# Layer 0 of a four-layer transformer stack: where the first norm runs, where the context's products stand, and what the last maxima are read from

## The chip, the cores and the metric

The kernel runs on one core of one Trainium2 chip. The metric is the device time of one execution in microseconds, the median of several runs. A core has a matrix engine (TensorE, PE in the profile; PEld is its weight load), VectorE (DVE), ScalarE (ACT), GpSimd (POOL) and SyncE (SP), whose queue issues most DMAs. Each takes its own instructions in order, and they wait for each other through semaphores.

## The reference

Eight samples of 256 tokens with 320 channels pass through four layers. The change is in layer 0 alone:

```python
h = attention(layer_norm(x, ln1_g, ln1_b), layer_norm(x, ln1_g, ln1_b), Wq1, Wk1, Wv1, Wo1, bo1, heads)
x = x + h
h = attention(layer_norm(x, ln2_g, ln2_b), ctx, Wq2, Wk2, Wv2, Wo2, bo2, heads)
x = x + h
x = x + geglu_ff(layer_norm(x, ln3_g, ln3_b), Wff1, bff1, Wff2, bff2)

def attention(x, ctx, Wq, Wk, Wv, Wo, bo, heads):
    q, k, v = fq_sym(x @ Wq), fq_sym(ctx @ Wk), fq_sym(ctx @ Wv)   # then 20 heads of 16
    w = fq_zero(softmax(q k^T * dh ** -0.5))
    return (w v, heads merged) @ Wo + bo
```

`fq_sym(x)` divides by `max(abs(x)) / 127`, rounds, and multiplies again; the maximum is over the whole tensor, all eight samples. `fq_zero` does the same with `max(w) / 255`. So within each attention nothing can be rounded before the last sample's queries and keys are projected, and no weight can be rounded before the last sample's softmax is known.

## The kernel before

Everything is held on the core. A sample is 2 tiles of 128 tokens. Each attention of layer 0 is a `Quant` object (`s` for self, `c` for cross) and goes through these passes:

- Projections. `project_all` (L1207) for `s`; `keys_all`, `values_all` (L1273) and `queries_all` (L1284) for `c`. After each product, ACT copies it from PSUM to SBUF, and `top` (L1201) has DVE reduce the largest absolute value into a column of `am`. For the last sample, `before` reads these maxima from PSUM in pieces; `am` has two more columns for them.
- `steps` (L1319), the first barrier of an attention. DVE reduces `am`; `all_max` (L485) goes over the partitions by two small transposes on PE (L489, L495) with DVE in between; then the step sizes follow.
- `whole` (L1339) rounds a sample's queries and keys: tk (L1347) and tq (L1350) scale and add 1.5*2^23, then L1353 and L1357 subtract it again and write two masked copies of the keys, and L1363 or L1365 the queries. With `fast` (sample 0, and sample 1 of `c`), DVE does the keys, GpSimd tq, and ACT the queries' last step; otherwise GpSimd does all.
- `tops_all` (L1407): scores on PE (L1422), their row maxima on DVE (L1425). `sums_all` (L1477): scores again, exponentials on ACT (L1473), sums on PE (L1488).
- `weight_steps` (L1514), the second barrier: the smallest sum over everything, by `all_max`, and a logarithm of all sums on ACT (L1518).
- `out_all` (L1547): `shift` (L1536) folds the sums into the row maxima; then, per group of heads, scores (L1466), exponentials, rounding on DVE (L1581), products with the values (L1563), and per sample the output projection and the addition to x (L483).

`weave` (L649) interleaves generators: each part has the round in which it begins, and every round takes one step of each living part. The order of an engine's instructions follows from this order of the program and from the framework, which takes work that is ready by its own model, the earliest in the program first. While `s.out_all()` runs, `c.queries_all()` normalises, turns and projects sample by sample (`norm`, `turn`, `project`), with the rounds of each sample in a table, `at`. The norm, `normed` (L296), takes statistics on DVE, a power on GpSimd (L310), and then L313, x minus mean times rstd, on DVE or on the engine given by `on`.

`context_steps` (L700) computes keys and values of the context for later layers and writes them to memory: a generator named `ahead`, each step a product with the context (L728), ACT copies into a staging tile, and DMAs on SP. The keys' staging tile, `kst`, has one buffer. One step is taken before `c.steps()`, 21 during `c`'s maxima and sums, at every second round (`paced`), and the rest during `c.out_all()`. PSUM offers three pairs of banks (`pair`) for all these products.

## Time and profile before

| | |
|---|---|
| median of 3 runs | 2235.7 us (2229.62 to 2238.51) |
| the profiled execution | 2235.43 us, its span 2233.4 us, mean granted clock 0.965 |
| self-attention: projections, then barrier | to 106, 106 to 110 us |
| its maxima and sums, barrier, output | 110 to 257, to 263, to 396 us |
| cross-attention: barrier, maxima and sums | 409 to 414, to 546 us |
| its barrier and output | to 553, to 675 us |
| all that follows (feed-forward, three layers) | 675 to 2233 us |

In the timeline a row has the start and the length in us, the engine, the line, the operation, what it writes and reads, how many instructions are merged, and in brackets the idle time of the engine before it and what ended it. In the windows a row has a stretch, the busy time of each engine in it with the number of instructions, the granted TensorE clock (1.00 is full speed), the DMA engines' share and GB/s.

### The profile page before, as it was taken

To read this page: it belongs to the slowest core of one execution; us is meant where nothing else is said; L and a number is where in the kernel's file an instruction comes from. 1 tells how busy PE (TensorE), PEld (TensorE's weight loads), DVE (VectorE), ACT (ScalarE), POOL (GpSimd) and SP (SyncE) were. 2 spreads that over 40 slices of the span, in tenths; PEclk is the share of its full clock that TensorE was granted. 3 is DMA by queue.
4 is the path that set the end of the run, shared out by engine and by line. 5 is a ranking of instruction groups with operands and counts; after the bars stand their busy time and mean duration, and the time that the engine had idled before them with its cause. 6 is when DMAs were issued, how large, how long until landed. Compare 5 with 4: busy or idle time off the path is not lost.

```text
span 2233.4 us, 38265 instructions
## 1 busy us (share of the span) xinstructions
PE 2044.5 (92%) x16413; PEld 1201.3 (54%) x16413; DVE 1117.4 (50%) x1698; ACT 825.7 (37%) x1252; POOL 357.9 (16%) x365
## 2 busy tenths in 40 slices
PE   6889878898899999999999999899999799999997
PEld 5643345554444555465555555554555455666664
DVE  4388677555752221335655667611121466556465
ACT  2347878467532121124444443411201233222221
POOL 1092066601411000000000001100000100000100
PEclk9989889898889999999999999999999899999999
DMA  4000000642110000020000001100000201000000
GB/s 117 17 12 2 1 1 4 167 111 57 55 53 28 1 0 1 1 92 2 2 2 22 27 25 35 47 1 0 1 1 2 68 25 32 12 24 26 23 19 16
DMA packets 79303, 63.21 MB, mean 28 GB/s; under 512 B 48410, under 2 KB 68318, under 8 KB 78622
## 3 DMA queue, kind: packets, MB, share of 16 engines
q1 hardware_dynamic: 75070, 57.06, 9.3%
q10 hardware_dynamic: 4064, 3.71, 0.6%
q8 instruction: 129, 2.11, 0.4%
q14 instruction: 40, 0.33, 0.1%
HBM read 42.61 MB, written 17.37 MB: 27 GB/s over the span
## 4 chain that ended last, share of the span: by engine, by line
PE 75%; DVE 16%; ACT 5%; issue 3%; DMA 1%; POOL 1%; SPq 0%; ACTq 0%; DVEq 0%; POOLq 0%
PE pf L120 13%; PE pf L584 13%; PE pf L132 9%; PE pa L120 7%; PE pa L447 6%; PE pf L430 4%; PE pa L584 3%; PE pf L139 3%; PE pf L385 3%; DVE negm L1425 3%; PE pf L1466 3%; PE pf L728 3%; DVE rs L455 2%; PE pa L1488 2%; DVE negm L392 2%
## 5 line engine op out<-in xcount | busy, mean ns | idle before, releaser
L436 ACT ACTIVATE e<-pf 128x1024 f32<-128x1024 f32 (+2 forms) x176 | 158.3, 944 | 234.9 <-PE pf L430 227.8
L392 DVE TENSOR_REDUCE negm<-pf 128x4 f32<-128x1024 f32 (+4 forms) x224 | 188.1, 886 | 108.8 <-PE pf L385 108.8
L584 PE MATMUL pf<-xTf,ff 128*128 128x512 f32 x512 | 232.4, 601 | 5.2 <-DVE negm L392 5.2
L455 DVE RECIPROCAL rs<-pa 128x256 f32<-128x256 f32 x88 | 152.2, 1745 | 144.0 <-PE pa L447 144.0
L477 POOL TENSOR_TENSOR xb<-x_sb,brow 128x640 f32<-128x640 f32 x40 | 62.2, 1555 | 792.2 <-DVE x_sb L483 748.2
L1473 ACT ACTIVATE e<-pf,sc_s 128x1024 f32<-128x1024 f32 x160 | 169.6, 1116 | 49.4 <-PE pf L1466 42.6
L1425 DVE TENSOR_REDUCE negm<-pf 128x4 f32<-128x1024 f32 (+2 forms) x128 | 143.3, 1134 | 68.1 <-PE pf L1422 61.4
L611 DVE SCALAR_TENSOR_TENSOR hT<-pf,cols_sb,gl 128x512 f32<-128x512 f32 x64 | 48.0, 751 | 256.8 <-ACT gl L610 254.5
L120 PE MATMUL pf<-ff,hT 128*128 128x320 f32 x640 | 174.4, 434 | 0.0
L584 PEld LDWEIGHTS pf<-xTf,ff 128*128 128x128 f32 x512 | 94.9, 191 | 125.2 <-issue 119.8
L120 PEld LDWEIGHTS pf<-ff,hT 128*128 128x128 f32 x640 | 120.9, 190 | 55.5 <-issue 6.1
L430 PE MATMUL pf<-qT,kT 32*128 32x256 f32 (+1 forms) x1280 | 122.3, 411 | 21.9 <-DMA qT<-nT 12.8
L610 ACT ACTIVATE gl<-pf,cols_sb 128x512 f32<-128x512 f32 x64 | 43.9, 687 | 248.0 <-PE pf L584 248.0
L385 PE MATMUL pf<-kT,qT 32*128 32x120 f32 (+1 forms) x1920 | 114.8, 329 | 18.3 <-ACT e L436 18.1
L120 PE MATMUL pa<-o,oT 128*128 128x320 f32 x352 | 105.4, 441 | 15.2 <-DVE oT L456 14.1
L385 PEld LDWEIGHTS pf<-kT,qT 32*128 32x128 f32 x1920 | 84.9, 189 | 58.4 <-ACT e L436 27.7
L1466 PE MATMUL pf<-Q,K 32*128 32x256 bf16 (+1 forms) x960 | 90.5, 294 | 25.3 <-DVE negm L1425 13.2
L639 POOL TENSOR_TENSOR xb<-x_sb,brow 128x640 f32<-128x640 f32 x16 | 25.1, 1566 | 543.1 <-DVE x_sb L644 528.7
L447 PE MATMUL pa<-e,v 128*32 128x256 f32 (+1 forms) x1280 | 105.2, 388 | 2.3 <-ACT e L436 1.7
L1581 DVE TENSOR_SCALAR w<-e 128x1024 bf16<-128x1024 f32 (+2 forms) x128 | 87.4, 691 | 37.5 <-ACT e L1473 36.3
L430 PEld LDWEIGHTS pf<-qT,kT 32*128 32x128 f32 (+1 forms) x1280 | 68.7, 183 | 68.3 <-issue 37.3
L132 PE MATMUL pf<-xT,q 128*128 128x256 f32 x384 | 101.0, 392 | 0.4 <-ACT e L436 0.2
(287 smaller groups left out, 3448.1 us busy)
## 6 DMA issues: line engine op xcount, KB each, us to landing
ff<-in_L_xattn_Wff_dram SPq DMA_DIRECT2D x1, 2560.0 KB
qT<-nT SPq DMA_DIRECT2D x160, 4.0 KB
ff<-in_L_xattn_ff_w_dram SPq DMA_DIRECT2D x1, 2560.0 KB
out_dram<-x_sb SPq DMA_DIRECT2D x16, 160.0 KB
kd_cross<-kst SPq DMA_DIRECT2D x8, 300.0 KB
vd_cross<-vst SPq DMA_DIRECT2D x8, 300.0 KB
vd_both<-vst SPq DMA_DIRECT2D x8, 300.0 KB
kT<-kd_cross SPq DMA_DIRECT2D x8, 300.0 KB
```

What stands on the lines that cost most here:

```text
L120: self.nc.tensor.matmul(out, l, r, start=i == 0, stop=i == len(pairs) - 1)
L132: self.nc.tensor.matmul(o, *t[c], start=start and c == 0, stop=stop and c == n - 1, skip_group_check=True)
L385: nc.tensor.matmul(s[j // 2][:, j % 2, o : o + nk], qT[r : r + PAD, g, t * P : (t + 1) * P], kT[r : r + PAD, g, :nk], start=True, stop=True,)
L392: nc.vector.tensor_reduce(negm[:, n, 2 * i : 2 * i + 2, g0 : g0 + len(gs), :].rearrange("p j g t -> p j (g t)"), sv[:, :, :, k0:k1], AX.X, ...
L430: nc.tensor.matmul(s[j // 2][:ks, j % 2, o : o + N], kT[r : r + PAD, g, c * ks : (c + 1) * ks], qT[r : r + PAD, g, :], start=True, stop=True,)
L436: nc.scalar.activation(e[:ks, 2 * i : 2 * i + 2, :n], s[i][:ks, :, :n], AF.Exp, scale=scale)
L447: nc.tensor.matmul(o[j * PAD : (j + 1) * PAD, what * N : (what + 1) * N], w, es[g][:ks, j, c * N : (c + 1) * N], start=first and c == 0 an ...
L455: nc.vector.reciprocal(rs, o[:, N:])
L584: ins = nc.tensor.matmul(*args, **kw)
L1425: nc.vector.tensor_reduce(negm[:, 2 * h : 2 * h + 2, gs[0] : gs[-1] + 1, :].rearrange("p j g t -> p j (g t)"), s[:, :, : len(gs) * TPB * n ...
L1466: nc.tensor.matmul(s[at // 2][:ks, at % 2, o : o + N], l, m, start=not shift and o == 0, stop=shift and o + N == n, skip_group_check=True,)
L1473: nc.scalar.activation(e[:ks, :, :n], ps[:ks, :, :n], AF.Exp, scale=self.sc[:ks, 9:10])
```

## The change

- In `queries_all`, the norm of sample 0 goes to DVE (before, only the last sample's did). All samples have the same rounds, five apart, so the last two no longer overlap, and the pass has 44 rounds instead of 40.
- The maxima of the last sample are taken from the SBUF copies, like the others'; `am` has 8 columns instead of 10.
- In `whole`, tk is always GpSimd's; with `fast`, DVE does tq and the queries' last step, and ACT and the constant `magic` are no longer used. Only sample 0 is fast.
- In `out_all`, the last values are taken one group per round, and the last sample's output in two rounds instead of one.
- Two steps of `c.values_all()` are taken after `s.weight_steps()`, ahead of the output pass; three follow from round 44 (before: from round 41), and three, not five, in `c`'s maxima.
- A second step of `ahead` is taken between `c.steps()` and `c.whole(0)`, and 20 instead of 21 in the weave that follows.

```diff
         def norm(b):
-            x[b] = k.normed(b, self.ln, on=nc.gpsimd if b + 1 < B else None)
+            x[b] = k.normed(b, self.ln, on=nc.gpsimd if 0 < b < B - 1 else None)
...
-            if b + 1 == B:
-                self.top(0, b + m, ps[:, 0, :N])
-            elif m == 2:
+            if m == 2:
                 self.top(0, b, self.q[b])
...
-        at = {b: [5 * b + i for i in (0, 3, 6, 7, 8)] for b in range(B - 2)}
-        at[B - 2] = [5 * B - 10 + i for i in (0, 3, 4, 5, 7)]
-        at[B - 1] = [5 * B - 10 + i for i in (3, 6, 7, 8, 9)]
-        for r in range(5 * B):
+        todo = {0: norm, 3: turn, 6: lambda b: project(b, 0), 7: lambda b: project(b, 1), 8: lambda b: project(b, 2)}
+        for r in range(5 * B + 4):
...
-            if b + 1 < B:
-                self.top(0, b, q)
-                self.top(1, b, kt)
-                continue
-
-            for i, ps in enumerate((pq, pk)):
-                self.top(i, b, ps[:, :, :N])
-            for i, ps in enumerate((pq, pk)):
-                self.top(i, B, ps[:, i, N:])
+            self.top(0, b, q)
+            self.top(1, b, kt)
...
-        to.tensor_scalar(tk[:, : 3 * nk], kt, sc[:, 7:8], MAGIC, ALU.mult, ALU.add)
+        nc.gpsimd.tensor_scalar(tk[:, : 3 * nk], kt, sc[:, 7:8], MAGIC, ALU.mult, ALU.add)
...
-        nc.gpsimd.tensor_scalar(tq, q, sc[:, 6:7], MAGIC, ALU.mult, ALU.add)
+        to.tensor_scalar(tq, q, sc[:, 6:7], MAGIC, ALU.mult, ALU.add)
...
-        if fast:
-            nc.scalar.activation(qh.rearrange("p c n -> p (c n)"), tq, AF.Identity, bias=k.magic)
-        else:
-            to.tensor_scalar(qh.rearrange("p c n -> p (c n)"), tq, MAGIC, None, ALU.subtract)
+        to.tensor_scalar(qh.rearrange("p c n -> p (c n)"), tq, MAGIC, None, ALU.subtract)
...
-            for _ in self.whole(b, self.cross and b == 1):
+            for _ in self.whole(b):
...
-        for r in range(rounds * B + 2):
+        for r in range(rounds * B + 4):
...
-            while len(todo) > (2 if b < B else 0):
+            if len(todo) > (2 if b < B else 0):
                 values(*todo.pop(0))
...
-                if r == rounds * B + 1:
-                    d, left = B, 0
...
-                k.weave((0, s.out_all()), (8, c.queries_all()), (5 * B + 1, islice(v, 3)))
+                for _ in range(2):
+                    next(v)
+                k.weave((0, s.out_all()), (8, c.queries_all()), (5 * B + 4, islice(v, 3)))
...
             c.steps()
+            next(ahead)
             for _ in c.whole(0, True):
                 pass
...
-                (1, k.paced(islice(ahead, 21), 1)),
+                (1, k.paced(islice(ahead, 20), 1)),
```

More of the change, by code (lines that the diff above doesn't have):

```diff
@@ L181, in open_quant @@
             nc.gpsimd.memset(self.place[:, g, 15 + g : 30 : G], 1.0)
-        self.magic = pool.tile([P, 1], F32, name="magic")
-        nc.gpsimd.memset(self.magic, -MAGIC)
         self.fill = pool.tile([P, 1], F32, name="fill")
@@ L1194, in __init__ @@
         n = "c" if cross else "s"
-        self.am = pool.tile([P, 3, B + 2], F32, name=f"am_{n}")
+        self.am = pool.tile([P, 3, B], F32, name=f"am_{n}")
         nc.gpsimd.memset(self.am, 0.0)
@@ L1202, in top @@
         self.k.nc.vector.tensor_reduce(
-            self.am[: src.shape[0], i, b : b + 1], src, AX.XY if len(src.shape) > 2 else AX.X, ALU.max,
-            apply_absolute_value=True,
+            self.am[: src.shape[0], i, b : b + 1], src, AX.XY if i == 2 else AX.X, ALU.max, apply_absolute_value=True
         )
@@ L1300, in project @@
             nc.scalar.copy(self.q[b][:, m * N : (m + 1) * N], ps[:, 0, :N])
-            if b + 1 == B:
-                self.top(0, b + m, ps[:, 0, :N])
-            elif m == 2:
+            if m == 2:
                 self.top(0, b, self.q[b])
-        at = {b: [5 * b + i for i in (0, 3, 6, 7, 8)] for b in range(B - 2)}
-        at[B - 2] = [5 * B - 10 + i for i in (0, 3, 4, 5, 7)]
-        at[B - 1] = [5 * B - 10 + i for i in (3, 6, 7, 8, 9)]
-        for r in range(5 * B):
+        todo = {0: norm, 3: turn, 6: lambda b: project(b, 0), 7: lambda b: project(b, 1), 8: lambda b: project(b, 2)}
+        for r in range(5 * B + 4):
             for b in range(B):
-                for i, n in enumerate(at[b]):
-                    if n == r:
-                        norm(b) if i == 0 else turn(b) if i == 1 else project(b, i - 2)
+                if r - 5 * b in todo:
+                    todo[r - 5 * b](b)
             yield
@@ L1520, in weight_steps @@
         least = k.small.tile([P, 1], F32, tag="least", name="least")
-        nc.vector.tensor_reduce(least, self.am[:, 0, :B], AX.X, ALU.min)
+        nc.vector.tensor_reduce(least, self.am[:, 0, :], AX.X, ALU.min)
         nc.vector.reciprocal(part[:, 0:1], least)
@@ L1524, in weight_steps @@
         if self.cross:
-            nc.vector.tensor_reduce(part[:, 1:2], self.am[:, 2, :B], AX.X, ALU.max)
+            nc.vector.tensor_reduce(part[:, 1:2], self.am[:, 2, :], AX.X, ALU.max)
             k.all_max(most, part)
```

## The prediction

> **What bounds the kernel now.** I read the page, then the chain of waits, then the timeline around the three barriers of layer 0, where a maximum over all partitions must be known before the next pass can start. The page first: what is the bound, and where does the granted clock fall?

> ```profile
> span 2233.4 us, 38265 instructions
> ...
> PE 2044.5 (92%) x16413; PEld 1201.3 (54%) x16413; DVE 1117.4 (50%) x1698; ACT 825.7 (37%) x1252; POOL 357.9 (16%) x365
> ...
> PEclk9989889898889999999999999999999899999999
> ```

> PE is busy 92% of the span and 75% of the chain. Everything the diff touches ends by 675 us, so the other 1558 us stay. Two stretches before that hold PE back. The first is in the timeline of the first attention's output pass:

> ```profile
> 290.59 6.66 POOL L313 TENSOR_SCALAR xh<-x_sb,mv,rstd 128x320 f32<-128x320 f32 x2
> ...
> 297.31 1.33 PE L330 MATMUL pf<-ident,xh 128*128 128x128 f32 x5 [2.77 <-POOL xh L313]
> ...
> 300.79 2.12 ACT L1473 ACTIVATE e<-pf,sc_s 128x1024 f32<-128x1024 f32 x2
> ...
> 301.93 0.69 DVE L1581 TENSOR_SCALAR w<-e 128x1024 bf16<-128x1024 f32 x1 [5.91 <-ACT e L1473]
> ...
> 396.88 0.45 DVE L313 TENSOR_SCALAR xh<-x_sb,mv,rstd 128x320 f32<-128x320 f32 x1 [0.82 <-POOL rstd L310]
> ```

> The norm of sample 0 takes 6.66 us on GpSimd; PE stands before its transposes and everything queued behind them, and ACT and DVE run dry. The same instruction on DVE takes 0.45 us (last row). The chain has these 6.67 us. The second stretch is the start of the cross-attention's maxima (two views: windows, columns after the length are PE, PEld, DVE, ACT, POOL busy, granted clock, DMA share, GB/s; then the timeline):

> ```profile
> 412.00:414.00 2.00, 0.00 (x0) 0.00 (x0) 2.00 (x7) 1.61 (x4) 1.78 (x2) 0.95 0.54 134
> ...
> 414.30:428.00 13.70, 11.59 (x65) 6.81 (x65) 6.00 (x10) 4.24 (x10) 13.19 (x12) 0.50 0.39 126
> ...
> 430.00:432.00 2.00, 2.00 (x10) 1.40 (x10) 0.66 (x2) 0.42 (x1) 2.00 (x3) 0.78 0.39 154
> ```

> ```profile
> 407.88 2.58 PE L728 MATMUL pf<-ctxT,ck 128*128 128x240 f32 x12
> ...
> 414.45 0.84 PE L1422 MATMUL pf<-K,Q 32*128 32x120 bf16 x16 [3.03 <-DVE K L1353]
> ...
> 415.22 4.96 PE L728 MATMUL pf<-ctxT,ck 128*128 128x240 f32 x12
> ...
> 421.95 4.96 PE L728 MATMUL pf<-ctxT,ck 128*128 128x240 f32 x12 [1.23 <-DVE negm L1425]
> ...
> 427.98 2.49 PE L120 MATMUL pf<-v,ctxT 128*120 128x320 f32 x4 [0.74 <-DVE negm L1425]
> ...
> 436.42 1.34 PE L120 MATMUL pf<-v,ctxT 128*120 128x320 f32 x4 [1.25 <-DVE negm L1425]
> ```

> After 3 us without work, PE runs at half clock from 414 to about 431: the 12 products of a key step take 4.96 us where they took 2.58 before. DVE and ACT wait for PE there, so this is PE's stretch.

> **Part 1, the first norm on DVE.** rstd is there at 290.48. Two L313 rows on DVE are 0.9 us, so the transposes can start near 292 instead of 294.1 and 297.3. Behind them ACT finishes its exponential at 294.4 and makes xT (2.03 us), so the next round's exponentials start at about 296.4, not 300.79: **-4.4**. [...] The rows say 3.3 us against 0.45, and I go by them. DVE is busy without a gap from 263 to 296, so its 0.9 us may come off the gain: -3.5 to -4.9.

> **Part 2, whole() for sample 0 (both passes).** The key's rounding moves to GpSimd; the query's two steps come to DVE from GpSimd and ACT. First attention: before, DVE did 0.62 + 1.15 + 1.00 (L1347, L1353, L1357) from 107.94 to 110.78, and the first score reduction started at 111.00. Now it does tq (0.62, by L1347), qh (1.15, by L1353 of the same size), kh 1.15 and 1.00: one operation more in the same queue, ahead of the reductions. **+1.1** (0.6 if qh fits into the 1.2 us in which GpSimd makes tk, 1.6 if all are slowed). The reductions follow each other every 1.13 us there and set the pace, so it passes on. Cross: 0.62 to 0.98 for tq, then 0.93 to 1.15 for qh, 0.92, 0.33 from 412.05: about 415.3 instead of 414.45, +0.85 (0.2 to 1.6), counted in part 4. Sample 1 of the cross pass goes wholly to GpSimd: 0.56 + 0.90 + 1.49 + 1.08 + 2.13 = 6.2 us behind sample 0's tk, done by 419.5; its scores are due at 428 at the earliest. GpSimd's queue then ends near 456 instead of 451.7, with each later sample needed well after it is made. Hidden; if the cover were gone it would be up to 5 us.

> **Part 3, two value products ahead of the output pass.** They fill PE's gap at 257 to 263 (1.27 us each), ahead of or between the two transposes of the maximum. That route has 0.7 us of slack, since ACT's logarithm ends at 260.4. Their copies (0.42) follow the logarithm and cost nothing; their maxima, 2 x 0.49 on DVE, are placed ahead of shift(0), the chain 260.53 to 263.29: **+0.8** (0 to 1.5). DMAs: none.

> **Part 4, a key step in the gap of c.steps.** It issues 12 matmuls, ACT's puts (2.7 us) and two kd_cross writes on SP. The matmuls fill 410.6 to 414; with a part before the second transpose, as where the same line lay around it at 547 (0.6 us later): **+0.5**. Behind SP's writes stand only loads for later layers. The kst tile has one buffer: bytes of the first step move until 415.0, so ACT's second puts run 415.2 to 417.9, and a step takes 2.7 + 2.1 = 4.85 us, the fourth done at 427.5 (in before, 435.6). Out of the stretch go one step at 4.96, two value products at 1.27 (2.5), and the half clock on what remains: the next step 4.96 to 2.58, scores 1.85 to 1.03, a value product 2.49 to 1.27, 0.3 of the fourth step, together 4.7. That is 12.2 of PE's time. Walked through with three PSUM pairs (a pair is free when ACT or DVE has read it), the score unit of 444.47 comes at 436.6, with a 2.0 us step more behind it: 7.9 + 2.0 = **-9.9**, the later start of 0.85 included (bounds -4 and -11.4). [...] The rows show half clock for 16 us at 85% busy, so I take 4.7.

> **Part 5, the last maxima from the copies, and the old round tables.** First attention: two reductions of 0.95 from the end of Q's copy at 103.9 end at 105.8; the four from PSUM ended at 105.86. 0. Second: one of 0.95 instead of 0.42 last, +0.53; the transpose L489 stood behind the first key step until 410.1 while its input was ready at 409.15, so the step hides it (uncovered: 0.53). The output pass drains one unit per round and the last two samples' queries no longer interleave: the same matmuls, with q(6,2) ahead of turn(7) rather than behind it, and a value product and the first key step to fill the 2 us of xT. **0** (-0.4 to +2). The second attention's output ends with the same order as before. The two rows of 128x30 and the magic constant go: 0.

> **Sum:** -4.4 + 1.1 + 0.8 + 0.5 - 9.9 + 0 = -11.9 us. The span of 2233.4 becomes 2221.5; what lies around it is 2.0 us, so the profiled 2235.43 becomes 2223.5. The median of the runs, 2235.7, is the same kernel within 0.3, so the forecast is **2223.5**.

> **Rivals.** (B) The gap is not filled: the framework may put the key step in front of the maximum's transpose, since it takes ready work first (it pulled L1466 ahead of a barrier at 256.6). The barrier then comes up to 2.6 later and PE idles as before: -4.4 + 2.4 - 4.96 + 2.6 - 2.5 + 0.85 = -6.0, 2229.5. For it: the order is not in the page. Against: at 546 the same line was placed between the two transposes. (C) The best case: part 1 at -4.9, part 2 at +0.6, nothing lost in part 3 and part 4 in full, -11.4: -15.7, 2220. For it: chain and windows show PE alone as the bound from 414 to 546. (D) Slower: ACT's second puts wait for the kst write, and behind them in ACT's queue the value copies; the PSUM pairs stay full and PE idles for 3 us, so the clock falls again. Each fall costs 8 to 9 us (half of some 17). One leaves -3.4, two give 2240.6, three 2249; it decides from the second on. For it: one kst buffer, three pairs. Against: no row of before waits for that write, whose bytes move within 2 us.

> **How the numbers follow.** Forecast 0.55, B 0.13, C 0.20, D 0.12. A change of 0.5% (11.2 us) is about what a measurement of this kernel can tell from none: below 2224.5 is faster, above 2246.9 slower. The forecast's own range is 2219 to 2229, 0.6 of it faster: 0.33, and C's 0.20, and a little of B: 0.55. Slower takes most of D: 0.09. The rest, 0.36, is same. The range reaches from the far side of C to that of D's middle: 2216 to 2238.

> **What would show it.** Part 1: L313 on DVE near 290.5 and no PE wait above 1 us before L330. Part 4: L728 within 410 to 414, granted clock 0.9 or more from 414 to 430, key steps of 2.6 us. Part 2: the first L1425 about 1.1 us later after its barrier. Wrong, if the clock is at 0.5 after 414 all the same, if L330 waits for a busy DVE, or if the tail from 390 to 410 grows by more than 2 us.

## The result and the profile after

| | before | after |
|---|---|---|
| median, 7 runs each | 2234.27 us (2229.62 to 2239.49) | 2224.31 us (2222.77 to 2226.72) |
| profiled execution, its span | 2235.43, 2233.4 us | 2225.48, 2223.4 us |
| mean granted clock | 0.965 | 0.965 |

The ratio is **0.9962** (95% interval 0.9947 to 0.9977): 0.38% faster, clear of zero, but inside the 0.5% that the prediction called "same" (it held "faster" to be likelier, at 0.55). Two later comparisons gave 0.9950 (0.9934 to 0.9966) and 0.9976 (0.9965 to 0.9988). Only ratios are compared between chips, since the kernel before had medians from 2228.8 to 2233.7 us in the later ones.

The page of the kernel after, busy time and granted clock over the span:

```profile
span 2223.4 us, 38256 instructions
...
PE 2046.0 (92%) x16413; PEld 1201.4 (54%) x16413; DVE 1121.6 (50%) x1695; ACT 822.7 (37%) x1249; POOL 359.6 (16%) x366
...
PEclk9989889898899999999999999999999899999999
```

PE still is the bound, and 10 us are gone. Where they went is read by marks: instructions that both traces have. "Step sizes" is the start of the last scaling in `steps`, "least sum" the first reduction of `weight_steps`, "first nTs product" the first product with nTs, the row maxima that `shift` has just made ready for the output pass. All stretches are of the two profiled executions; together they make up the 10.0 us.

| stretch | before | after | difference | predicted |
|---|---|---|---|---|
| start to the self step sizes | 107.82 | 105.88 | -1.9 | 0 |
| to the first score reduction (roundings) | 3.18 | 4.07 | +0.9 | +1.1 |
| to the least sum | 146.66 | 147.90 | +1.2 | 0 |
| to the first nTs product (barrier) | 5.68 | 6.56 | +0.9 | +0.8 |
| to the exponential behind xT (the norm) | 37.45 | 35.20 | -2.2 | -4.4 |
| to the cross step sizes | 111.14 | 112.20 | +1.1 | +0.5 |
| to the first cross scores (roundings) | 2.51 | 3.33 | +0.8 | +0.85 |
| to the least sum (maxima and sums) | 131.81 | 125.17 | -6.6 | -10.75 |
| to the first nTs product (barrier) | 6.15 | 6.15 | 0 | 0 |
| to the feed-forward (output pass) | 124.12 | 115.22 | -8.9 | 0 |
| to the end | 1556.85 | 1561.73 | +4.9 | 0 |

(In the prediction, the -9.9 of part 4 holds both the +0.85 and the -10.75.) The total came out near the forecast, but the largest entry was not predicted, and the largest prediction fell short. Two entries lie within what executions of one kernel differ by: the start took 105.49 us in a second execution of before, and the end 1555.6 to 1561.9 us in all 14 executions of this document, 1557.6 in the second one of before.

The timeline of the output pass after, where before GpSimd's norm held PE:

```profile
290.72 0.88 POOL L308 TENSOR_TENSOR rstd<-ve,nhalf 128x2 f32<-128x2 f32 x1 [0.83 <-DVE ve L306]
291.60 0.79 POOL L1352 TENSOR_SCALAR tv<-V,sc_s 128x640 f32<-128x640 f32 x1
291.64 2.21 DVE L311 TENSOR_SCALAR xh<-x_sb,mv,rstd 128x320 f32<-128x320 f32 x2 [0.61 <-POOL rstd L308]
...
293.78 1.37 DVE L1561 TENSOR_SCALAR w<-e 128x1024 bf16<-128x1024 f32 x2
294.50 0.40 PE L1543 MATMUL pa<-w,V 128*32 128x256 bf16 x2 [3.47 <-DVE w L1561]
...
294.55 3.12 ACT L1453 ACTIVATE e<-pf,sc_s 128x1024 f32<-128x1024 f32 x3 [4.17 <-DVE w L1561]
...
295.74 1.54 PE L328 MATMUL pf<-ident,xh 128*128 128x128 f32 x6
...
297.55 2.03 ACT L336 ACTIVATE xT<-pf,cols_sb 128x256 f32<-128x256 f32 x4
...
299.60 1.11 ACT L1453 ACTIVATE e<-pf,sc_s 128x1024 f32<-128x1024 f32 x1
```

The two norms take 2.21 us on DVE, not 6.66 on GpSimd, and nobody waits for xh any more. But DVE stood 0.61 us for rstd with the rounding of the weights queued behind, and PE now waits 3.47 us, ACT 4.17, for that rounding (w). xT comes behind ACT's exponentials, which so begin at 294.55 only.

The cross barrier's stretch after, windows, then PE's timeline:

```profile
411.00:414.30 3.30, 1.89 (x10) 1.11 (x9) 2.52 (x9) 1.63 (x5) 2.24 (x3) 1.00 0.71 229
414.30:417.70 3.40, 1.34 (x18) 1.03 (x19) 2.72 (x4) 2.13 (x6) 3.40 (x4) 0.50 0.53 137
417.70:421.10 3.40, 3.40 (x11) 2.02 (x10) 0.28 (x1) 0.25 (x2) 3.40 (x4) 0.50 0.80 268
...
431.30:434.80 3.50, 3.50 (x8) 1.77 (x8) 0.97 (x2) 2.55 (x7) 3.50 (x5) 0.51 0.70 126
```

```profile
411.21 1.68 PE L726 MATMUL pf<-ctxT,ck 64*128 64x240 f32 x8
415.13 0.61 PE L1402 MATMUL pf<-K,Q 32*128 32x120 bf16 x16 [2.24 <-DVE Q L1345]
416.96 4.96 PE L726 MATMUL pf<-ctxT,ck 128*128 128x240 f32 x12 [1.22 <-DVE negm L1405]
...
423.69 4.96 PE L726 MATMUL pf<-ctxT,ck 128*128 128x240 f32 x12 [1.23 <-DVE negm L1405]
...
432.00 3.30 PE L726 MATMUL pf<-cv,ctxT 128*120 128x320 f32 x8
```

The key step lies in the gap, as meant. PE is idle for 2.24 us behind it all the same, and the clock falls to 0.50 from 414.3 to 434.8, for 20 us (before: 17). The two steps that follow stand in the same rounds as in before, are as slow (4.96 us), and come no sooner: 416.96 and 423.69 us here, 415.22 and 421.95 there.

In the traces the granted clock changes only on a grid of 3.41 us: the shortest stretches at 0.50 last that long, the one from 414.29 us of after 20.48 us (6 steps), the one from 413.82 us of before 17.07 us (5 steps). The grid lies at another place against the program in most executions (0.01 to 2.50 us after the same product, by the table further down); below, "a fall of 4" is 4 steps of that grid at 0.50.

### The profile page after: what moved, and what is told of

Same layout as the page of the kernel before. It is cut to its first block, busy times and chain, and to the rows that moved or that the text cites. A ratio compares the mean times of both kernels' runs of the same rounds, so it can differ in the third digit from the quotient of the medians.

```text
span 2223.4 us, 38256 instructions
## 1 busy us (share of the span) xinstructions
PE 2046.0 (92%) x16413; PEld 1201.4 (54%) x16413; DVE 1121.6 (50%) x1695; ACT 822.7 (37%) x1249; POOL 359.6 (16%) x366
## 4 chain that ended last, share of the span: by engine, by line
PE 75%; DVE 15%; ACT 4%; issue 3%; DMA 2%; POOL 1%; SPq 0%; ACTq 0%; DVEq 0%; POOLq 0%
PE pf L582 13%; PE pf L120 13%; PE pf L132 9%; PE pa L120 7%; PE pa L445 6%; PE pf L428 4%; PE pa L582 3%; PE pf L383 3%; PE pf L139 3%; PE pf L1446 3%; PE pf L726 3%; DVE negm L1405 3%; DVE rs L453 2%; PE pa L1468 2%; DVE negm L390 2%
## 5 line engine op out<-in xcount | busy, mean ns | idle before, releaser
L453 DVE RECIPROCAL rs<-pa 128x256 f32<-128x256 f32 x88 | 152.2, 1745 | 144.4 <-PE pa L445 144.4
L475 POOL TENSOR_TENSOR xb<-x_sb,brow 128x640 f32<-128x640 f32 x40 | 62.3, 1558 | 801.4 <-DVE x_sb L481 758.8
L120 PE MATMUL pf<-ff,hT 128*128 128x320 f32 x640 | 174.4, 434 | 0.0
L120 PEld LDWEIGHTS pf<-ff,hT 128*128 128x128 f32 x640 | 120.9, 190 | 55.5 <-issue 6.1
L120 PE MATMUL pa<-o,oT 128*128 128x320 f32 x352 | 107.2, 446 | 15.2 <-DVE oT L454 14.1
```

The source lines that it names most:

```text
L120: self.nc.tensor.matmul(out, l, r, start=i == 0, stop=i == len(pairs) - 1)
L453: nc.vector.reciprocal(rs, o[:, N:])
```

## The experiments

**The same kernel again.** No edit.

> The changed kernel unchanged, to tell which of the differences between the two traces come with the edit. The granted clock changes only on a grid of 3.41 us whose phase against the program differed between the two executions (falls began 3.41 us times a whole number apart, and the two grids lay 0.09 of a step apart). Theory (chance): the clock falls at 622 and 646 us of before, which after does not have, and the one at 1750 are set by where the grid lies, so this execution has other short falls than the first one of the same kernel, and the stretch from the second sums to the feed-forward (121.4 us in the first) moves by several us while the code is the same. Rival (edit): it is 121.4 within 1 us again. Both: the median stays at 2224.3 within 3 us, and the fall after the cross barrier is there again.

Measured: median 2224.46 us, ratio 0.9950; 125.2 us for the cross maxima, 121.4 from the least sum to the feed-forward, with the same falls at the same distances. So this one execution speaks for "edit". In it the grid happened to lie as in the first one against the cross output pass (0.99 and 0.96 us, modulo 3.41); the table further down has other places.

**Part 1 undone.**

```diff
-            x[b] = k.normed(b, self.ln, on=nc.gpsimd if 0 < b < B - 1 else None)
+            x[b] = k.normed(b, self.ln, on=nc.gpsimd if b < B - 1 else None)
```

> The changed kernel with the first norm of the second pass back on GpSimd, nothing else: part 1 of the prediction by itself. My term: 4.4 us, so the exponentials behind the turn start some 2 to 4.4 us later after the barrier than the 35.2 us of after (37.5 in before). From the two traces the half of it is given back before the last query, since from the barrier to the steps of the cross-attention after gained 1.2 us only: so the whole kernel is 1 to 2 us slower than the changed one (2225.5 to 2226.5). Rival, all of the 4.4 kept: 2228.7. Rival, DVE is the bound in that stretch and GpSimd's norm costs nothing: 2224.3, and the exponentials at 35 us.

Measured: median 2226.27, 1.8 us above the changed kernel beside it (ratios 0.9969 and 0.9950, intervals overlapping). In its timeline the old wait is back:

```profile
290.05 6.66 POOL L311 TENSOR_SCALAR xh<-x_sb,mv,rstd 128x320 f32<-128x320 f32 x2
...
296.77 1.33 PE L328 MATMUL pf<-ident,xh 128*128 128x128 f32 x5 [2.77 <-POOL xh L311]
...
298.20 2.04 ACT L336 ACTIVATE xT<-pf,cols_sb 128x256 f32<-128x256 f32 x4 [4.63 <-PE pf L328]
```

From the nTs product to xT it takes 35.52 us against 33.15: **2.4 us**, and 2.6 at the cross step sizes. So part 1 is worth 2.4, and it is kept, contrary to my guess ahead of this run that half of it was given back: the +1.1 us of the next stretch is in this kernel too.

**The key step back in the weave.**

```diff
             c.steps()
-            next(ahead)
...
-                (1, k.paced(islice(ahead, 20), 1)),
+                (1, k.paced(islice(ahead, 21), 1)),
```

> The changed kernel with the key step between the two barriers left where it was (21 steps in the weave, none ahead of whole): the heart of part 4 by itself. My prediction's terms: step 4.96, half clock 4.7, barrier -0.5, so some 8 to 9 us slower than the changed kernel (2232 to 2233). From the trace of after, in which the clock fell all the same: the 4.96 of one half-clock step come back, less 0.1 at the barrier: 4 to 5.5 us slower (2228.5 to 2230). Rival, the step is hidden in the weave anyway, since its ACT puts and writes set the pace: 0 to 1 us (2224 to 2225.5). The stretch from the first cross scores to the least sum (125.2 us in after, 131.8 in before) tells them apart: 134, 130, 126.

Measured: median 2229.48, ratio 0.9984 (0.9963 to 1.0005), 5.0 us above the changed kernel, with intervals that just touch; the cross maxima take 132.6 us. That lies between the two expectations of 134 and 130, but not for either reason. Of the 48 score reductions of that pass, number 13 (from 0) is 36.9 us after the first scores (35.8 in after): the step is missing from the stretch behind the barrier, and that costs 1 us. A fall of 4 at 444.1 then costs 3.3 us up to number 40 (before, which has no step in the gap either, shows no such fall in two executions, so whether these are the step's is open), and 3.0 more are lost between reductions 40 and 42 (5.7 us against 2.7; 8.4 in before).

What happens there, in before (ACT's and PE's timeline) and then in after:

```profile
513.10 0.94 ACT L781 ACTIVATE vst<-pf,cols_sb 120x320 f32<-120x320 f32 x2 [0.67 <-PE pf L728]
...
518.99 0.36 ACT L804 ACTIVATE vst<-ident 128x192 f32<-128x192 f32 x1 [3.19 <-DMA vd_both<-vst]
519.26 1.00 ACT L360 ACTIVATE kst<-pf,m,half 128x256 f32<-128x256 f32 x2
...
520.57 0.68 PE L1466 MATMUL pf<-Q,K 32*120 32x256 bf16 x4 [1.92 <-ACT kst L364]
```

```profile
508.03 0.94 ACT L779 ACTIVATE vst<-pf,cols_sb 120x320 f32<-120x320 f32 x2
...
509.46 2.12 ACT L1453 ACTIVATE e<-pf,sc_c 120x1024 f32<-120x1024 f32 x2
512.54 0.36 ACT L802 ACTIVATE vst<-ident 128x192 f32<-128x192 f32 x1 [0.96 <-DMA vd_both<-vst]
```

In before, ACT clears the padding of a staging tile and has to wait 3.19 us for its last write to land; the copies behind it, which would empty PE's PSUM pair, stand too, PE waits 1.92 us, and the clock falls for 2. In after every later step of `ahead` comes one place earlier in the weave; the same write now runs while ACT makes two large exponentials, and 0.96 us of it is left. With the step back in the weave ACT waits 2.90 us and PE 1.63 at that place. All 14 executions agree: reductions 40 to 42 take 2.7 us in the ten with the step in the gap, and 4.6 to 8.6 us in the four without it.

**One step fewer in the weave, none in the gap.**

```diff
             c.steps()
-            next(ahead)
```

> The changed kernel without the key step in the gap, and with 20 steps in the weave all the same, so that one step more is left for the output pass. It asks where the gain of part 4 lay. In both traces the first steps of the weave start at the same places (415.2 and 421.9 us before, 417.0 and 423.7 after), so the step that the weave no longer has is its last, at round 41, near 519 us, where before PE waited 1.9 us for an ACT copy queued behind a write of vst, and two steps of the clock grid at 0.5 followed; unit 40 of 48 of the score reductions came 103.1 us after the first scores in before and 102.4 in after, unit 42 111.5 and 105.1. Theory (last step): first scores to least sum 125 to 127 us, as in after (without the key step it was 132.6), units 40 to 42 within 3 us, the output pass up to 2 us longer, the median 2225 to 2227. Rival (my prediction: the key step's place at 415 us is what counts): 130 to 132 us, and 2228.5 to 2230.

Measured: median 2239.84, ratio **1.0039** (1.0025 to 1.0053), the cross maxima 137.4 us. Both expectations missed. Leaving the last step out is not what helps: the wait is there again, in its timeline:

```profile
526.11 0.36 ACT L802 ACTIVATE vst<-ident 128x192 f32<-128x192 f32 x1 [3.49 <-DMA vd_both<-vst]
...
527.69 0.46 PE L1446 MATMUL pf<-Q,K 32*120 32x256 bf16 x2 [2.23 <-ACT kst L362]
```

and with it a fall of 4 at 526.9, beside falls of 5 at 444.9 and of 1 at 489.3. So what takes the wait away in after is, by these two runs, the shift of every later step by one place, which only the step ahead of the weave brings.

**Idle products in the gap.** `warm(k, n)` issues n products of 128x480 of the identity with the context into a bank that nobody reads (two instructions each in the profile).

```diff
-            next(ahead)
+            next(ahead), warm(k, 5)
...
-                                )
+                                ); self.cross and b == 0 and n + t + j == len(gs) + 1 and warm(k, 2)
```

> The changed kernel with products that nobody reads, on a bank of their own, put where PE stands still behind the cross barrier: 5 of 128x480 (an estimate of 0.48 us each at full clock, from the 0.32 us of a 320-column product) between the key step and the first scores, 2 after each of the six score units of sample 0. It tests the term that failed: what makes the clock fall to 0.5 at 414 us. Theory (filling): the clock goes by how full PE was in the 3.41 us before; the key step alone left PE idle for 2.2 us of 3.4; with the products it stays at 1.00 from 414 to 430, key steps take 2.6 us, and in spite of 17 idle products this stretch is 4 to 5.5 us shorter (2219 to 2220.5). Rival (kind of work or event): the clock falls there whatever PE does, the products run at 0.95 us each and make it 6 to 9 us slower (2230 to 2233). A fall one step of the grid later, since PE waits 1.2 us for DVE after the first scores, would give 2223 to 2226.

Measured: median 2226.61, ratio 0.9985 (0.9967 to 1.0004). The clock stays at 1.00 from 299 to 544 us, so in this run filling held it. But a product took 0.94 us, twice my estimate, and 17 of them fill 16 us: the first scores come 1.7 us later, the cross maxima take 124.7 us, and the output pass has a fall of 4 and two of 1 (123.1 us). The size was not tested; hence:

**Fewer of them**: `warm(k, 2)` in the gap and `warm(k, 1)` after each unit.

> As the run with idle products, which kept the clock at 1.00 from 302 to 544 us, with fewer of them: 2 ahead of the first scores and 1 after each of the six units (a product of 128x480 turned out to take 0.94 us, so its 17 filled 16 us). 8 products are 7.5 us, of which the gap takes 1.9. Theory (the half clock costs 4 to 5 us here): the clock stays at 1.00 again, the first scores come 3.3 to 3.6 us after the step sizes, unit 13 of the reductions at 31 to 32 us after them instead of 35.8, and the kernel ends near 2219 to 2221 if no other fall comes in its place. Rival (DVE, ACT and the writes set the pace of this stretch, not PE): the clock is 1.00, and unit 13 comes at 34 to 36 all the same: 2223 to 2225. Third (too few products): it falls at 414 to 418 us, unit 13 comes at 37 to 40, 2226 to 2229.

Measured: ratio 0.9981 (0.9962 to 1.0000), median 2221.80. Its windows behind the barrier and PE's timeline (the columns as above):

```profile
411.00:414.40 3.40, 2.76 (x15) 0.94 (x13) 2.79 (x5) 0.71 (x2) 3.40 (x4) 1.00 0.82 276
414.40:417.80 3.40, 3.40 (x22) 2.04 (x21) 1.61 (x2) 1.68 (x5) 3.40 (x4) 1.00 0.60 209
...
428.10:431.50 3.40, 3.40 (x28) 1.89 (x29) 1.83 (x3) 1.43 (x7) 3.40 (x4) 1.00 0.85 231
```

```profile
410.85 1.77 PE L1778 MATMUL pa<-ctxT,ident 128*128 128x480 f32 x4
413.27 0.38 PE L1402 MATMUL pf<-K,Q 32*128 32x120 bf16 x8 [0.64 <-DVE Q L1345]
...
415.81 2.58 PE L726 MATMUL pf<-ctxT,ck 128*128 128x240 f32 x12
...
420.86 2.58 PE L726 MATMUL pf<-ctxT,ck 128*128 128x240 f32 x12
```

Full clock, key steps of 2.58 instead of 4.96 us, the first scores not later (3.34 us), and PE busy for 81% or more of every window. Reduction 13 comes 29.9 us after the first scores instead of 35.8, the maxima end after **120.2** us instead of 125.2. So 5.0 us are to be had there, net of the six idle products behind the gap: the forecast had 4.7.

**The value products undone.**

```diff
-                for _ in range(2):
-                    next(v)
```

> The changed kernel without the two value products ahead of the output pass (three of them then come in its last rounds as before, five in the maxima of the cross-attention). My terms: 0.8 to 0.9 us at the barrier come back, and two products of 1.27 us go into the stretch from 435 us: 1.6 us slower (2226). Rival, they are hidden in that stretch: 0.9 us faster (2223.4). Least sum to first nTs product 5.7 instead of 6.56 in both; first scores to least sum 127.5 or 125.2.

Measured: the barrier goes back to 5.68 us, which settles the 0.88. The rest of the question stays open: the maxima took 144.4 us and the median was 2229.0 (ratio 1.0015, 0.9991 to 1.0038), but the two products themselves put reduction 13 only 0.3 us later; then a fall of 11 begins at 452.2. This profiled execution took 2239.69 us, 10.7 above the median, so its fall need not be in the others. The windows of it:

```profile
452.20:470.00 17.80, 17.80 (x104) 9.15 (x105) 4.36 (x8) 7.64 (x17) 3.19 (x3) 0.50 0.27 79
470.00:489.70 19.70, 19.70 (x116) 10.24 (x116) 5.11 (x7) 9.05 (x18) 0.00 (x0) 0.50 0.27 54
```

PE is busy without a gap at half clock for 37 us. Four waits of 0.3 to 0.5 us for ACT and DVE, within 445 to 451 us, stand ahead of it; why the full rate then stays away is not known.

**The kernel before again.** No edit.

> The kernel before, unchanged, for another place of the 3.41 us grid on which the clock changes. The cross output pass took 124.1 us from its first nTs product to the feed-forward with falls at 611.8, 622.0 and 645.9 us, and 114.3 to 115.5 in four executions of the changed kernel and its variants without them, but 123.1 with them in the run with idle products, whose code there is the same. Theory (chance): the boundaries of the grid lay 0.3 to 1.1 us (modulo 3.41) after that first product where there was no fall and 1.4 to 1.8 where there was; in this execution the pass takes 114 to 116 or 123 to 125 by where the grid lies. Rival (edit): 124 within 1 us wherever it lies.

Measured: 123.7 us for the cross output pass, falls of 4 at 623.0 and of 1 at 612.7 and 646.9. The grid lay 1.44 us after the first nTs product, on the side where a fall was expected. All 14 profiled executions, by that place:

| grid boundary after the pass's first nTs product, modulo 3.41 us | output pass | of it at half clock | executions |
|---|---|---|---|
| 0.01 to 1.17 us | 114.3 to 115.5 us | 17 to 22 us | after three times, 5 of its variants |
| 1.35, 1.44 us | 124.1, 123.7 us | 36 us | before, twice |
| 1.72 to 2.50 us | 119.9 to 125.0 us | 30 to 37 us | 4 variants |

Nearly the same stretch of the pass, before and after, in windows:

```profile
610.00:620.00 10.00, 9.01 (x75) 5.13 (x74) 5.01 (x13) 6.32 (x8) 0.00 (x0) 0.83 0.56 179
620.00:630.00 10.00, 9.48 (x40) 3.73 (x32) 5.31 (x12) 3.49 (x4) 2.23 (x2) 0.60 0.00 0
```

```profile
603.00:613.00 10.00, 8.56 (x85) 5.19 (x87) 6.09 (x16) 7.34 (x12) 2.23 (x2) 1.00 0.46 138
613.00:623.00 10.00, 8.92 (x68) 4.17 (x65) 7.12 (x16) 4.05 (x5) 2.24 (x2) 1.00 0.11 41
```

All 12 executions of the changed kernel and its variants have the same code in that pass (but for one step of `ahead` more in one of them) and yet take about 115 or 120 to 125 us: the 8.9 us are those falls, and in these executions they go by the place of the grid. The change touched the end of this pass too (last values and last output), but two variants with the changed code and the falls of before (1, 4 and 1) took 123.1 us against 124.1 and 123.7: that leaves 1 us at most for the edit. Whether before can land on the good side, and how often unprofiled runs do, two executions of it don't tell.

**Four kernels side by side**: the changed one, the 8 idle products, the old roundings, and both.

> The changed kernel unchanged, as the common measure for the three that follow. Both theories: 0.995 to 0.9965 of the kernel before, as in the two comparisons so far; first cross scores to least sum 125.2 us with the fall behind the barrier, and the cross output pass 115 or 124 us by where the clock's grid lies.

> The run with 8 idle products again, now beside the changed kernel on one chip: whether the 5.0 us that its trace gained in the cross maxima (120.2 instead of 125.2 us) are there in the time. Theory (the half clock behind the barrier costs 5 us): 4 to 6 us below the changed kernel. Rival (a fall avoided there is followed by others, as the cross output pass had falls in its first execution): within 2 us of it.

```diff
-        nc.gpsimd.tensor_scalar(tk[:, : 3 * nk], kt, sc[:, 7:8], MAGIC, ALU.mult, ALU.add)
+        to.tensor_scalar(tk[:, : 3 * nk], kt, sc[:, 7:8], MAGIC, ALU.mult, ALU.add)
...
-        to.tensor_scalar(tq, q, sc[:, 6:7], MAGIC, ALU.mult, ALU.add)
+        nc.gpsimd.tensor_scalar(tq, q, sc[:, 6:7], MAGIC, ALU.mult, ALU.add)
...
-        to.tensor_scalar(qh.rearrange("p c n -> p (c n)"), tq, MAGIC, None, ALU.subtract)
+        if fast:
+            nc.scalar.activation(qh.rearrange("p c n -> p (c n)"), tq, AF.Identity, bias=k.magic)
...
-            for _ in self.whole(b):
+            for _ in self.whole(b, self.cross and b == 1):
```

> The changed kernel with the roundings of sample 0 as before (keys on DVE, query's scaling on GpSimd, its last step on ACT, sample 1 of the cross pass on DVE too): part 2 by itself. My terms: 1.1 us at the self barrier and 0.85 at the cross barrier come back, so about 1.9 us faster than the changed kernel; the traces showed 0.89 and 0.82, so 1.7. Rival (the first reductions wait for something else): 0. Third: PE's gap behind the key step shrinks from 2.2 to 1.4 us, so the clock may stay at 1.00 there, which brings 5 us more.

> Both at once: the roundings as before, with 1 idle product ahead of the first cross scores and 1 after each of the first six units. If the two gains are of different things (0.82 and 0.89 at the barriers, 5.0 by the clock), it is 6 to 7 us below the changed kernel, and the best of all so far. Rival (the earlier scores already keep the clock up): no better than the roundings alone.

The medians are of 22, 6, 15 and 12 runs.

| | median | ratio to before | self, cross roundings | cross maxima | output pass |
|---|---|---|---|---|---|
| changed kernel | 2226.61 us | 0.9976 (0.9965 to 0.9988) | 4.07, 3.34 us | 125.3 us | 115.3 us |
| 8 idle products | 2217.41 us | 0.9939 (0.9917 to 0.9961) | 4.07, 3.34 us | 121.7 us | 115.4 us |
| old roundings | 2223.77 us | 0.9962 (0.9945 to 0.9978) | 3.19, 2.52 us | 126.6 us | 123.1 us |
| both | 2219.24 us | 0.9946 (0.9922 to 0.9970) | 3.18, 2.52 us | 129.0 us | 114.9 us |

With 8 idle products the kernel is 9 us below the changed one, more than the expected 4 to 6, with intervals that don't overlap; its trace shows 3.6 us in the maxima (a fall of 1 at 439.7), so not all of the 9 is placed, and in its first comparison it had 0.9981, no better than the changed kernel has. By the one comparison in which they stood side by side it beats both kernels. The old roundings bring back 0.88 and 0.82 us, exactly the two differences of the marks; in the time, 2.8 us with overlapping intervals. The shorter gap didn't keep the clock up by itself (a fall of 5 at 414.5). Both together were not the best: no fall at 414, but one of 6 at 440.1.

## Why the prediction was right, and where it was wrong

The time was right to 0.8 us (2223.5 against 2224.3), in part by luck: the output pass gave 8.9 us that no step had, the start 1.9 (its first products began at 18.2 us instead of 20.1), and 1.2 and 4.9 were taken back where no code was changed: of the clock's grid, 6 steps at 0.50 instead of 4 lie between 137 and 176 us, and 5 instead of 2 between 676 and 1700 us, at an estimated 1.7 us each, half of a step of 3.41 us, if PE is the bound. The stretches whose difference a run has tied to the edit (roundings, self barrier, norm, key step, cross maxima) sum to some -6.3 us; by their ratios, the two later comparisons measured about -11 and -5 us.

**Part 1** (-4.4, range -3.5 to -4.9): right in kind, too large; 2.4 us by the run that undoes it. The mis-sized term is "two L313 rows on DVE are 0.9 us": they took 2.21, with GpSimd at work beside them, after 0.61 us in which DVE's queue stood for rstd. That is 1.3 and 0.6 of the missing 2.0 us, which reached xT through w and ACT. It is the sign named in the forecast, a PE that waits for a busy DVE, only for w and not for xh.

**Part 2** (+1.1 and +0.85): right, 0.88 and 0.82, by undoing. **Part 3** (+0.8): right, 0.88 at the barrier; the 2.5 us that the two products were to give back behind 435 us were not seen (0.3). **Part 5** (0): the last maxima end 1.8 us after the copy of Q, before 2.0; in the cross pass the first transpose starts 2.22 us after the first key step in both. The +1.1 us between the norm and the cross steps is mostly clock: its fall lasts to 301.6 us, 2.0 us past the mark at 299.60, in before only 0.4 past 300.79. In the run with 17 idle products, whose code is the same up to there, the fall ended at the mark, and the stretch took 111.3 us, in before 111.1.

**Part 4** (-9.9 with the later start, -5.8 measured) failed in two steps. First, "the half clock on what remains ... together 4.7": the size was good (5.0 by the trace of the 8 idle products), but the premise, that a key step fills the gap and keeps the clock up, was not. In the grid step from 410.87 to 414.28 PE had 2.0 us of work out of 3.4, and the clock fell: the first sign of being wrong that the prediction named. Second, "Out of the stretch go one step at 4.96": it doesn't go out. The weave takes one step every second round whichever it is, so steps 3 and 4 stand where 2 and 3 stood. Up to reduction 40, at 518 us, after had gained 0.7 us (102.4 against 103.1); the other 5.7 to 6 came from the wait at 519 us and its fall, which I had not read from before's timeline. The +0.5 at the barrier was 0.1: from the reduction of `am` to the step sizes it takes 2.58 us, and 2.46 without the step. Nor did one grid step full of work bring the clock back: PE was busy without a gap from 417.7 to 421.1 us, and the clock stayed at 0.50 until 434.8.

**The rivals.** B asked the right question, whether the gap is filled, but for a wrong place of the step; the step was in the gap and the clock fell. Of D, the wait for kst is there (2.94 us, ACT at 415.57) while PE's waits there name DVE; no second fall followed.

**Not foreseen**: the cross output pass, whose code the change touched only at its end. Which falls it had went, in the 14 executions, by the place of the grid (0.01 to 1.17 us: 114.3 to 115.5 us; 1.35 to 2.50: 119.9 to 125.0); a forecast of this kernel within 0.4% has to leave some 9 us for that alone.

## What to carry to other kernels

A step moved ahead of a loop that takes one step per so many rounds leaves the loop's beginning as it is; look at which round loses its step, and at what each later one now stands beside. A gap in PE cost more than its length here: 3.03 us without work in before and 2.24 in after were followed by 17 and 20 us at half clock. Filling a part of it was not enough (59% of the step from 410.87 to 414.28 in after); the fullest step of 3.41 us that a fall followed was 80% busy. With 8 products that nobody reads PE was busy for 81% or more of every window from 411.0 to 431.5 us, and the clock stayed at 1.00 there; they gained 5.0 and 3.6 us in the traces, and in the time in one of two comparisons. Before a difference of some 0.4% is put down to an edit, sum the time at half clock stretch by stretch, in more than one execution.
